# A state-space stage on one core: side work a unit ahead, the product with C written in place

## The chip, the cores and the metric

The kernel runs on one core of one Trainium2 chip. The metric is the time of one execution on the device, in microseconds (us). The core has five engines that run side by side, each taking its instructions strictly in order: TensorE (PE, with its weight loads as PEld), VectorE (DVE), ScalarE (ACT), GpSimd (POOL) and SyncE (SP), which here issues nearly all transfers. They wait for one another through semaphores.

## The reference, cut to what matters

The whole model has four layers. The change touches only the first, a two-level selective state-space block (x is 4 images of 96 channels and 64 x 64 pixels, so sequences of L = 4096; DIN = 192, DSTATE = 16, NLAYERS = 2):

```
for i in range(NLAYERS):
    seq = seq + mamba(seq, ...)
# in mamba, with h the normalized input:
xs, z = split(h @ in_w)
xc    = silu(conv4(xs))                      # causal, 4 taps
dt, Bm, Cm = split(xc @ xproj_w)             # 6, 16, 16 columns
delta = softplus(dt @ dt_w + dt_b)
dA    = exp(delta[..., None] * -exp(A_log))  # L x 192 x 16
dBx   = delta[..., None] * Bm[:, :, None, :] * xc[..., None]
h_t   = dA_t * h_(t-1) + dBx_t               # a scan along L
y     = (einsum('blds,bls->bld', h, Cm) + Dp * xc) * silu(z)
return y @ out_w
```

A fusion by matmul, a batch norm and the residual follow, and then the three other layers (`_back`), whose code is not touched.

## The kernel before, in words

`_mamba` cuts the sequences into chunks of TC = 512 positions. A **unit** is (chunk, level, pair of images), 32 in all, in a fixed list in which a level-1 unit comes three places after the level-0 unit that it reads (units 2 and 31 excepted; they are in `late`, because their input is made only one or two units earlier).

The scan of a unit has 24 **steps** (k, r, h): k = 0..2, r = 0..3, h = 0..1, so step = 8k + 2r + h. Each step treats 2 x 128 rows of (channel, state) pairs, 512 positions long. The loop over the steps writes out by hand, for each engine, the order of its instructions (`manual_schedule`); nothing reorders them later. In step s it issues, in this order:

- `product(s+2)` (line 457, on POOL) if step s+2 is **apart**, that is k < 2, h = 0 and r odd: steps 2, 6, 10 and 14 of a unit. There the input term is loaded (`db`) and multiplied by B on POOL. Then `broadcasts(s+2)` (line 447): otherwise PE spreads delta times x over the states into PSUM (`pq`, three buffers of two banks).
- `reduce` (line 488) in odd steps: PE sums h times C over the states of the step pair finished before, into `py`.
- a **slot** of side work (below).
- `decays(s+3)` (line 452): ACT computes dA = exp(delta A) into tile `a` (six buffers); for an apart step, into `pq`.
- `scans(s)` (line 470): two DVE scans of 512, with DVE's `product(s+1)` (line 457, pq times B) between them unless step s+1 is apart; then POOL's product of the states with C (line 476), from tile `hs` (two buffers, one for each pair of steps) into tile `hc` (two buffers).
- `copies(s+5)` (line 434): SP's transfers of delta, broadcast over 16 partitions of states, from DRAM (`ddl`) into `a`.
- `states` (line 480) in even steps: ACT copies the last column of `hs` to a small tile `hst`, the start of the next chunk's scan. `gate` every 8 steps: y (lines 496, DVE, and 497, POOL).

The **side work** is everything that makes the next units ready. It is a set of Python generators in lanes (class `Side`, lanes front, tail, norm, rest); one call of `slot` lets a lane issue work up to its next `yield`. `yield` alone ends the slot and keeps the lane, "free" lets other lanes in, "gap" asks for at least one slot's distance. `tail(n-1)` projects the finished unit (mm_o, line 369 on), `norm(n+2)` normalizes the input (mm_xc, mm_v, 12 tiny POOL instructions for a reciprocal square root at line 227 on, mm_r at line 240, DVE's `hn` at line 249), and `front(n+1)` is the long chain: mm_i (line 264), Silu, mm_dbl (line 287), three ACT copies (dbl, dh, and dh rounded at line 297), `dx` on POOL (line 303), mm_d, Softplus (line 601), `ddl` to DRAM, `du` on POOL (line 339), copies `ux`/`uy` on ACT (line 352), remainders `ul` on POOL (line 355) and their transfers. All side matmuls share one PSUM bank (`mm`), so each group waits until the group before is copied out.

In the kernel before, `front(n+1)` begins at step 0 of unit n and must be finished at its end: `copies` calls slots in a loop until the next unit is ready, and at step 23 `side.drain()` empties all lanes. In an ordinary unit there is one slot in each step; unit 0 and units before a `late` one have two.

Of the kernel before, what the change touches and what calls it, by code (L numbers as in the profile page):

```python
# [9 lines left out]
F32 = mybir.dt.float32  # L10
# [13 lines left out]
NL = 2  # L24
DS = 16
# [23 lines left out]
def _mamba(ctx, tc, io, w, fd, fstats, xsums):  # L49
# [25 lines left out]

    A, HS, HC = ("a", 0, 2, 6), ("hs", 0, 4, 2), ("hc", 0, 4, 2)

# [10 lines left out]
    fus_w = _load(nc, wp, io["fus_wT"][0:C, :], [C, C], "fus_w")  # L88
    out_wT = staged(io["out_wT"], "out_wT", [C, 2, 128], *HC)
    selF = staged(io["k_sel"].rearrange("c (j m) -> c j m", j=4), "selF", [128, 4, 128], *A)  # L90
# [10 lines left out]

    dtH = stage("dtH", [128, NL, 256], *HC)
    nc.vector.tensor_copy(dtH.bitcast(F32R), dtF)
# [64 lines left out]

    seq, made, ys = {}, {}, {}
    pqs, das, dbs, hss, hcs, pys = {}, {}, {}, {}, {}, {}  # L170

# [17 lines left out]
    def norm(unit):  # L189
# [47 lines left out]
        for n, b in enumerate(bs):  # L237
            p = mm(f"r{n}", unit, [C, TC])
            for j in range(4):
                nc.tensor.matmul(  # L240
                    p[:, j * 128 : (j + 1) * 128],
                    r[:, n * 4 + j : n * 4 + j + 1].to_broadcast([128, C]),
                    ident,
                    start=True,
                    stop=True,
                )
            yield
            yield
            nc.vector.tensor_tensor(hn_buf[b, l][:C, 3:], p, xc[n], ALU.mult)
            yield "free"  # L250

    def front(unit):

        ch, l, pr = unit
        bs = (2 * pr, 2 * pr + 1)
        for j in range(6):
            k = j % 3
            p = mm(f"i{j}", unit)
            taps = [(wk[l][:, t, :], t) for t in range(4)] if j < 3 else [(wz[l], 3)]
            for t, (wt, off) in enumerate(taps):  # L260
                cols = slice(off, off + TC)
                f = dict(start=t == 0, stop=t + 1 == len(taps))
                if k < 2:
                    nc.tensor.matmul(p, wt[:, 0:128], hn_buf[bs[k], l][:, cols], **f)  # L264
                else:
                    for n in range(2):
                        nc.tensor.matmul(p[64 * n : 64 * n + 64], wt[:, 128:DIN], hn_buf[bs[n], l][:, cols], **f)
                if t != 0 and t != 2 or len(taps) == 1:
                    yield
            if j == 0:  # L270
                xcv = tl("xcv", unit, [128, 3, TC], bufs=2)
            if j == 3:
                zs = tl("zs", unit, [128, 3, TC], bufs=2)
            if j < 3:
                nc.scalar.activation(xcv[:, j, :], p, AF.Identity, bias=col(l, 0, k))  # L275
            else:
                nc.scalar.copy(zs[:, k, :], p)
            yield "free"
# [23 lines left out]
        dx = tl("dx", unit, [128, TC], F32R)  # L302
        nc.gpsimd.tensor_tensor(dx, dbl, lo, ALU.add)  # L303
        yield "gap"
        dl = tl("dl", unit, [128, 3, TC])
        bcs = []
        for k in range(3):
# [7 lines left out]
            nc.scalar.activation(dl[:, k, :], p, AF.Identity, bias=col(l, 1, k))  # L315
            if k == 1:
                for at in range(2):
                    t = tl(f"bc{at}", unit, [128, 2, TC], bufs=2)
                    src = ddb[at].rearrange("s n t -> s (n t)")[:, None].to_broadcast([DS, 8, 2 * TC])
                    nc.sync.dma_start(t.rearrange("p n t -> p (n t)"), src)  # L320
                    bcs.append(t)
        _softplus(nc, work, dl)
# [3 lines left out]
        for q in range(4):  # L326
            nc.sync.dma_start(dd[q % 2, :, :, q // 2, :], dl[32 * q : 32 * q + 32])
        us, parts, dus, cut = [], [], [], []
        made[unit] = [xcv, zs, *bcs, dd, us, parts]
        for at in range(6):  # L330
            if at == 2:
                for k in range(2):
# [3 lines left out]
                    us.append(ddu)  # L336
            for k in ((0, 1), (2,))[at] if at < 2 else ():
                dus.append(tl(f"du{k}", unit, [128, TC], to="du", bufs=3))
                nc.gpsimd.tensor_tensor(dus[k], dl[:, k, :], xcv[:, k, :], ALU.mult)
            if at >= 3:  # L340
# [5 lines left out]
                parts.append(cut[at - 3][0:2])  # L346
            while at == 3 and side.step < NS * units.index(unit) - 3:
                yield "gap"
            if 1 <= at < 4:
                cut.append([tl(f"{x}{at}", unit, [128, TC], F32R, to=x, bufs=3) for x in ("ux", "uy")])  # L350
                for t in cut[-1]:
                    nc.scalar.copy(t, dus[at - 1])
            if 2 <= at < 5:
                t = tl(f"ul{at}", unit, [128, TC], F32R, to="ul", bufs=2)
                nc.gpsimd.tensor_tensor(t, dus[at - 2], cut[at - 2][0].bitcast(F32), ALU.subtract)
                cut[at - 2].append(t)
            yield "gap"

    def tail(unit):
# [4 lines left out]
        for n in range(2):  # L364
# [13 lines left out]
            else:  # L378
                ft = work.tile([C, TC], F32, name=f"ft_{tag(unit)}_{n}", tag="ft", bufs=2)
                nc.scalar.copy(ft, p)  # L380
# [5 lines left out]
    def way_out(unit):  # L386
# [11 lines left out]
        for n in range(2):  # L398
            b = 2 * pr + n
            nc.vector.bn_stats(fstats[:, b, ch, :], po[:C, n, :])  # L400
            ft = work.tile([C, TC], F32, name=f"ft_{tag(unit)}_{n}", tag="ft", bufs=2)
            nc.scalar.copy(ft, po[:C, n, :])
# [56 lines left out]
    def scans(s):  # L459
# [3 lines left out]
        if h == 0:  # L463
            hss[g] = scan.tile([128, 4, TC], F32, name=f"hs_{name(s)}", tag="hs")
            hcs[g] = scan.tile([128, 4, TC], F32, name=f"hc_{name(s)}", tag="hc")
        pq, a = pqs.pop(s), das.pop(s)
        d0, d1 = (pq, dbs.pop(s)) if apart(s) else (a, pq)
        for i in (0, 1):
            at = 2 * h + i
            nc.vector.tensor_tensor_scan(  # L470
                hss[g][:, at, :], d0[:, i, :], d1[:, i, :], hst[pr, l, g % 12][:, at : at + 1], ALU.mult, ALU.add
            )
            if i == 0 and s + 1 < n_steps and not apart(s + 1):
                product(s + 1)
        sl = slice(2 * h, 2 * h + 2)
        (nc.gpsimd if s + 1 < n_steps else nc.vector).tensor_tensor(hcs[g][:, sl, :], hss[g][:, sl, :], bc(unit, 3, k, h), ALU.mult)  # L476

    def states(g):
        ch, l, pr = steps[2 * g][0]
        nc.scalar.copy(hst[pr, l, g % 12], hss[g][:, :, TC - 1])  # L480

    def reduce(g):
        unit, k, r, h = steps[2 * g]
        if r == 0:
            pys[unit, k] = ps_y.tile([128, TC], F32, name=f"py_{name(2 * g)}", tag="py")
        hc = hcs.pop(g)
        for i in range(4):
            nc.tensor.matmul(  # L488
                pys[unit, k][32 * (i // 2 + i % 2 * 2) :][:32], red[:, r, :], hc[:, i, :], start=(r == 0), stop=(r == 3)
            )  # L490
# [9 lines left out]
    class Side:  # L500
# [5 lines left out]
        def __init__(self):  # L506
            self.front, self.tail, self.norm, self.rest, self.held, self.step = [], [], [], [], None, 0

        def slot(self):
            waiting = []  # L510
            while True:
                lane = self.held
                if lane is None:
                    lanes = (self.front, self.tail, [] if self.tail else self.norm, self.rest)
                    lanes = [x for x in lanes if x and not any(x is y for y in waiting)]
# [9 lines left out]
                elif got == "end":  # L525
                    lane.pop(0)

        def drain(self):
            while self.slot():
                pass  # L530

    side = Side()
    n_steps = len(steps)
    with tc.manual_schedule():
        for n in (0, 1):
            load(units[n])
        side.front = [weights(0), norm(units[0]), front(units[0])]
        side.drain()
        for s in range(5):
            copies(s)  # L540
# [6 lines left out]
        for s in range(n_steps + NS):  # L547
# [5 lines left out]
            if at == 0:  # L553
                if n + 1 < len(units) and n + 1 not in late:
                    side.front += ([norm(units[n + 1])] if n == 0 else []) + [front(units[n + 1])]
                    side.norm += [weights(1)] * (n == 0)
            if at == 22 and n + 1 == len(units):
# [6 lines left out]
            if n + 2 < len(units) and n + 2 not in late:  # L564
                if at == 8:
                    load(units[n + 2])
                if at == 10:
                    (side.front if n + 1 in late else side.norm).append(norm(units[n + 2]))
            if s + 2 < n_steps:
                unit, k, r, h = steps[s + 2]  # L570
# [9 lines left out]
            side.slot()  # L580
            if n == 0 or n + 1 in late:
                side.slot()
            if s + 3 < n_steps and not apart(s + 3):
                decays(s + 3)
            if live:
                scans(s)
            if live and s + 5 < n_steps:
                unit, k, r, h = steps[s + 5]
                while unit not in made or apart(s + 5) and len(made[unit][5]) <= k:
                    side.slot()  # L590
                copies(s + 5)
            if s % 2 == 0 and 0 < s <= n_steps:
                states(s // 2 - 1)
            if s % 8 == 2 and 2 < s <= n_steps + 2:
                gate(s // 2 - 2)
            if at == NS - 1 and n + 1 < len(units):
                side.drain()

# [955 lines left out]
```

## Time and profile before

| | us |
|---|---|
| three runs before | 5245.57, 5257.07, 5259.77 (median 5257.07) |
| the profiled execution | 5239.08 |
| its span, first to last instruction | 5237.3 |
| before the first scan / the state-space steps / all that follows | 93 / 2991 / 2153 |
| busy in the state-space steps: DVE, POOL, PE, ACT | 2666.7, 2549.8, 2207.8, 1782.6 |
| mean granted clock of TensorE, whole span | 0.819 of full speed |

A unit is 48 scans. In the profile a row such as "L470 DVE TENSOR_TENSOR_SCAN hs<-a,hst,pq ... x1280 | 1575.0, 1263 | 40.1 <-ACT hst L480 17.3" says: line 470 of the kernel, on VectorE, writes hs from a, hst and pq, 1280 times; 1575.0 us busy, 1263 ns each; VectorE was idle for 40.1 us just before these, and most of that ended when ScalarE's line 480 was done. Rows of a timeline are start, duration, engine, line, operation, tiles, count, and in brackets the idle time before with what ended it. Rows of stretches are the stretch, its length, each engine's busy time (with its number of instructions), TensorE's granted clock, the share of the transfer engines that was busy, and GB/s.

### The profile page before, as it was taken

To read this page: it belongs to the slowest core of one execution; us is meant where nothing else is said; L and a number is where in the kernel's file an instruction comes from. 1 tells how busy PE (TensorE), PEld (TensorE's weight loads), DVE (VectorE), ACT (ScalarE), POOL (GpSimd) and SP (SyncE) were. 2 spreads that over 40 slices of the span, in tenths; PEclk is the share of its full clock that TensorE was granted. 3 is DMA by queue.
4 is the path that set the end of the run, shared out by engine and by line. 5 is a ranking of instruction groups with operands and counts; after the bars stand their busy time and mean duration, and the time that the engine had idled before them with its cause. 6 is when DMAs were issued, how large, how long until landed. Compare 5 with 4: busy or idle time off the path is not lost.

```text
span 5237.3 us, 52687 instructions
## 1 busy us (share of the span) xinstructions
PE 4069.8 (78%) x15440; PEld 1747.5 (33%) x15440; DVE 4322.3 (83%) x5639; ACT 2693.7 (51%) x5149; POOL 2988.1 (57%) x2105
## 2 busy tenths in 40 slices
PE   5677777777777777777777637899898899989776
PEld 2222222222222222222222102345455555545565
DVE  2879899898989989899998887879787978787655
ACT  3565666656566665656656520024453544434566
POOL 2878888888888888888888860002130312212122
PEclk7767877777787777778787658999999999999977
DMA  4768888888887888888788765553325233332110
GB/s 100 179 168 192 197 193 205 195 197 195 197 195 192 209 196 193 195 197 202 186 208 196 175 168 157 165 174 94 95 86 155 85 98 97 100 90 79 53 33 21
DMA packets 314046, 800.19 MB, mean 153 GB/s; under 512 B 52247, under 2 KB 58106, under 8 KB 312702
## 3 DMA queue, kind: packets, MB, share of 16 engines
q1 hardware_dynamic: 310174, 790.53, 59.8%
q10 hardware_dynamic: 3584, 6.29, 0.4%
q8 instruction: 123, 2.02, 0.2%
q14 instruction: 165, 1.35, 0.1%
HBM read 703.83 MB, written 67.63 MB: 147 GB/s over the span
## 4 chain that ended last, share of the span: by engine, by line
PE 26%; DVE 24%; issue 15%; POOL 11%; ACT 9%; DMA 7%; SPq 1%; DVEq 0%; POOLq 0%; ACTq 0%
DVE hs L470 10%; PE py L895 10%; DVE pq L457 6%; DMA a<-ddl 5%; POOL hc L476 4%; PE py L488 2%; DVE z L880 2%; ACT a L452 2%; DVE a L1110 2%; PE px L1177 2%; PE ph L1092 2%; PE pa L1078 2%; PE mm_i L264 2%; POOL t L1248 1%; PE pv L1133 1%
## 5 line engine op out<-in xcount | busy, mean ns | idle before, releaser
L476 POOL TENSOR_TENSOR hc<-hs,bc 128x1024 f32<-128x1024 f32 x767 | 1803.2, 2360 | 318.4 <-DVE hs L470 305.7
L470 DVE TENSOR_TENSOR_SCAN hs<-a,hst,pq 128x512 f32<-128x512 f32 x1280 | 1575.0, 1263 | 40.1 <-ACT hst L480 17.3
L895 PE MATMUL py<-z,wk 128*96 128x512 f32 x2304 | 1113.1, 612 | 25.0 <-issue 14.0
L452 ACT ACTIVATE a<-a,aneg 128x512 f32<-128x512 f32 x1280 | 846.1, 711 | 223.4 <-DMA a<-ddl 216.1
L880 DVE TENSOR_TENSOR z<-cp,cp 128x512 f32<-128x512 f32 x1152 | 794.9, 717 | 183.7 <-PE py L895 169.0
L457 DVE TENSOR_TENSOR pq<-pq,bc 128x1024 f32<-128x1024 f32 x640 | 773.2, 1208 | 111.6 <-PE pq L447 111.5
L488 PE MATMUL py<-hc,red 128*32 128x512 f32 x3072 | 672.3, 840 | 39.4 <-POOL hc L476 39.4
L895 PEld LDWEIGHTS py<-z,wk 128*96 128x96 f32 x2304 | 366.9, 169 | 448.7 <-issue 318.9
L447 PE MATMUL pq<-uy,sel 64*128 64x512 f32 x768 | 262.9, 643 | 281.1 <-DVE hs L470 275.1
L470 DVE TENSOR_TENSOR_SCAN hs<-pq,hst,db 128x512 f32<-128x512 f32 x256 | 325.5, 1271 | 148.1 <-POOL dx L303 95.0
L1145 POOL MEMSET zz<- 96x2 f32 x16 | 1.6, 98 | 738.5 <-ACT zz L1154 738.5
L264 PE MATMUL mm_i<-hn,wk 97*128 97x512 f32 x512 | 297.7, 710 | 118.3 <-ACT xcv L275 93.2
L1246 POOL TENSOR_TENSOR o<-o,fb 128x384 f16<-128x384 f16 x64 | 67.0, 1047 | 547.1 <-ACT o L1251 544.1
L452 ACT ACTIVATE pq<-a,aneg 128x512 f32<-128x512 f32 x256 | 177.0, 692 | 343.5 <-DMA a<-ddl 249.3
L457 POOL TENSOR_TENSOR db<-db,bc 128x1024 f32<-128x1024 f32 x128 | 302.0, 2360 | 23.8 <-DMA db<-ddu 23.8
L447 PEld LDWEIGHTS pq<-uy,sel 64*128 64x128 f32 x768 | 97.9, 234 | 568.4 <-DVE hs L470 431.7
L447 PE MATMUL pq<-ux,sel 64*128 64x512 f32 x512 | 181.5, 635 | 96.4 <-DVE hs L470 76.6
L275 ACT ACTIVATE xcv<-mm_i,pvec 128x512 f32<-128x512 f32 x96 | 66.0, 687 | 313.1 <-PE mm_i L264 147.8
L1177 PE MATMUL px<-bd,a 128*96 128x128 f32 x1024 | 148.2, 293 | 67.1 <-DVE a L1110 56.2
L1146 POOL TENSOR_TENSOR zz<-zz 96x256 f32<-96x256 f32 x128 | 122.8, 959 | 133.4 <-ACT zz L1153 81.3
L264 PEld LDWEIGHTS mm_i<-hn,wk 97*128 97x128 f32 x512 | 98.7, 214 | 291.1 <-issue 165.5
L447 PEld LDWEIGHTS pq<-ux,sel 64*128 64x128 f32 x512 | 66.9, 231 | 305.3 <-DVE hs L470 212.0
(286 smaller groups left out, 6534.3 us busy)
## 6 DMA issues: line engine op xcount, KB each, us to landing
a<-ddl SPq DMA_DIRECT2D x768, 512.0 KB, 6.8
cp<-p SPq DMA_DIRECT2D x480, 192.0 KB, 2.7
db<-ddu SPq DMA_DIRECT2D x128, 512.0 KB, 9.0
bc<-ddb SPq DMA_DIRECT2D x64, 512.0 KB, 7.8
cp<-p SPq DMA_DIRECT2D x480, 64.0 KB, 2.7
ddl<-dl SPq DMA_DIRECT2D x128, 192.0 KB, 3.9
tw_k_fwd<-in_k_fwd SPq DMA_DIRECT2D x64, 256.0 KB, 3.4
tw_k_inv<-in_k_inv SPq DMA_DIRECT2D x64, 256.0 KB, 3.1
```

The source lines that it names most:

```text
L264: nc.tensor.matmul(p, wt[:, 0:128], hn_buf[bs[k], l][:, cols], **f)
L447: nc.tensor.matmul(pqs[s][:, i, :], sel[rows, r, :], made[unit][6][k][h][rows], start=True, stop=True)
L452: nc.scalar.activation(to[:, i, :], das[s][:, i, :], AF.Exp, scale=acol(s, i))
L457: engine.tensor_tensor(t, t, bc(unit, 2, k, h), ALU.mult)
L470: nc.vector.tensor_tensor_scan(hss[g][:, at, :], d0[:, i, :], d1[:, i, :], hst[pr, l, g % 12][:, at : at + 1], ALU.mult, ALU.add)
L476: (nc.gpsimd if s + 1 < n_steps else nc.vector).tensor_tensor(hcs[g][:, sl, :], hss[g][:, sl, :], bc(unit, 3, k, h), ALU.mult)
L488: nc.tensor.matmul(pys[unit, k][32 * (i // 2 + i % 2 * 2) :][:32], red[:, r, :], hc[:, i, :], start=(r == 0), stop=(r == 3))
L880: nc.vector.tensor_tensor(zs[n], cps[q, r0], cps[q, r1], ALU.mult)
L895: nc.tensor.matmul(pys[q], wk[k // KG][:, k % KG, :], zs.pop(n), start=(k == 0), stop=(k == NE - 1))
L1078: nc.tensor.matmul(pa[j][:, jj, :], kf[:, 2 * (j % 2) + jj, :], dd[j][:, jj, :], start=True, stop=True)
L1146: nc.gpsimd.tensor_tensor(z0[:, :, 0, :], z0[:, :, 0, :], z1[:, :, 0, :], ALU.add)
L1177: nc.tensor.matmul(p[:, j, :], a2[i % 2][:, kk, :], tabs["bd"][:, int(kk > 0), :], start=True, stop=True)
```

## The change

1. **In place.** `hs` gets 513 columns and three buffers, `hc` is gone. The scans write columns 1 to 512; POOL's product with C reads these and writes columns 0 to 511 of the same tile. The last state stays in column 512 for `states`; `reduce` reads columns 0 to 511.
2. **A unit ahead.** `front(n+2)` is started in unit n, in a new lane `ahead` behind all others, from step 4 on, as soon as both images of `norm(n+2)` are done (`normed`); at the unit's end the lane becomes `front`. Loads and norms start at steps 2 and 4 instead of 8 and 10. `xcv` and `zs` get a third buffer. `side.drain()` at step 23 is gone, and odd steps have two slots.
3. **The chain's last part** (ux, uy, ul, their transfers, bc and ddu) is a generator of its own, `split`, in a lane `low` that goes first, and is spread over the unit before the one that needs it (from its steps 2, 5, 13 and 21).
4. **dx behind the product.** `dx` is not issued at once but put into `side.post` and issued (`flush`) at the next slot or after the step's product with C.
5. `copies` catch up in a loop that remembers how far it came. The tail's ft tiles share sq's buffers.

```diff
+            hss[g] = scan.tile([128, 4, TC + 1], F32, name=f"hs_{name(s)}", tag="hs", bufs=3)
-            hcs[g] = scan.tile([128, 4, TC], F32, name=f"hc_{name(s)}", tag="hc")
...
-                hss[g][:, at, :], d0[:, i, :], d1[:, i, :], hst[pr, l, g % 12][:, at : at + 1], ALU.mult, ALU.add
+                hss[g][:, at, 1:], d0[:, i, :], d1[:, i, :], hst[pr, l, g % 12][:, at : at + 1], ALU.mult, ALU.add
...
-        (nc.gpsimd if s + 1 < n_steps else nc.vector).tensor_tensor(hcs[g][:, sl, :], hss[g][:, sl, :], bc(unit, 3, k, h), ALU.mult)
+        hs = hss[g][:, 2 * h : 2 * h + 2, :]
+        (nc.gpsimd if s + 1 < n_steps else nc.vector).tensor_tensor(hs[:, :, :TC], hs[:, :, 1:], bc(unit, 3, k, h), ALU.mult)
...
     def front(unit):
+        while unit not in normed:
+            yield "gap"
...
-                xcv = tl("xcv", unit, [128, 3, TC], bufs=2)
+                xcv = tl("xcv", unit, [128, 3, TC], bufs=3)
...
-        nc.gpsimd.tensor_tensor(dx, dbl, lo, ALU.add)
+        side.post.append(lambda: nc.gpsimd.tensor_tensor(dx, dbl, lo, ALU.add))
...
+        while side.low:
+            yield "gap"
+        for ks in ((0, 1), (2,)):
+            for k in ks:
+                dus.append(tl(f"du{k}", unit, [128, TC], to="du", bufs=3))
+                nc.gpsimd.tensor_tensor(dus[k], dl[:, k, :], xcv[:, k, :], ALU.mult)
+            if len(ks) == 2:
+                yield "gap"
+        side.low.append(split(unit, ddb, dus, us, parts))
+
+    def split(unit, ddb, dus, us, parts):
+        cut, start = [], NS * units.index(unit) - NS
+        while side.step < start + 2:
+            yield "gap"
...
-            while at == 3 and side.step < NS * units.index(unit) - 3:
+            while at < 4 and side.step < start + 8 * at - 3:
                 yield "gap"
...
-                    lanes = (self.front, self.tail, [] if self.tail else self.norm, self.rest)
+                    lanes = (self.low, self.tail, self.rest, self.front, [] if self.tail else self.norm, self.ahead)
...
+    copied = [5]
...
             if at == 0:
-                if n + 1 < len(units) and n + 1 not in late:
-                    side.front += ([norm(units[n + 1])] if n == 0 else []) + [front(units[n + 1])]
+                side.turn()
...
-                if at == 10:
+                if at == 4:
                     (side.front if n + 1 in late else side.norm).append(norm(units[n + 2]))
+                    side.ahead.append(front(units[n + 2]))
...
-            if n == 0 or n + 1 in late:
+            if n == 0 or n + 1 in late or s % 2 == 1:
                 side.slot()
...
             if live:
                 scans(s)
-            if live and s + 5 < n_steps:
-                unit, k, r, h = steps[s + 5]
-                while unit not in made or apart(s + 5) and len(made[unit][5]) <= k:
+            side.flush()
+            while live and copied[0] < min(s + 6, n_steps):
+                unit, k, r, h = steps[copied[0]]
+                while unit not in made or apart(copied[0]) and len(made[unit][5]) <= k:
+                    if copied[0] > s + 5:
+                        break
                     side.slot()
-                copies(s + 5)
+                else:
+                    copies(copied[0])
+                    copied[0] += 1
+                    continue
+                break
...
-            if at == NS - 1 and n + 1 < len(units):
-                side.drain()
```

The instructions of the two kernels are the same in kind and number on DVE, ACT and POOL; what differs is their order, the tiles and the waits. The steady order of one unit, as it stands on the engines in the changed kernel (steps of unit n; mm_o is of unit n-1; mm_xc to mm_dbl, mm_d, dx, Softplus and du are of unit n+2; ux, uy and ul of unit n+1):

| steps | PE side work | ACT side work | POOL side work |
|---|---|---|---|
| 3, 4 | mm_o, mm_o, mm_xc | copies of both mm_o | y at step 2 |
| 5 to 8 | mm_xc, mm_v | xc, sq, ux, uy, ve, vh, r | Newton (12 small) after step 6's product |
| 9, 10 | mm_r, mm_r | | y (hn on DVE at the end of steps 9 and 10) |
| 11 to 18 | mm_i | xcv, ux, uy, zs, both Silu | ul after step 12's product, y |
| 19 to 21 | mm_dbl, mm_d, mm_d | dbl, dh, dh, ux, uy, dl | dx, ul after step 20's product |
| 22 to 24 | mm_d | dl, dl, Softplus | ul, du, du after step 22's, du before step 24's |

In the kernel before, mm_r stood at steps 21 and 23, mm_i at 0 to 8, mm_o at 9 and 10, both Silu and their table loads between these, mm_dbl at 11 and 12, mm_d at 14 to 16, Softplus at 17, du at 17 and 18, the Newton steps after step 18's product, and ul after the products of steps 19, 20 and 22.

## The prediction

> **What bounds the kernel now.** I read the stretches first. The stretch 400 to 2800 holds the steady units. The columns are its length, the busy time of PE, PEld, DVE, ACT and POOL with instruction counts, TensorE's granted clock, the transfer engines' share and GB/s; the second row counts the scans (line 470) alone, the third those of the start.
>
> ```profile
> 400.00:2800.00 2400.00, 1809.03 (x6116) 564.68 (x6114) 2168.12 (x1927) 1468.77 (x2552) 2086.53 (x1303) 0.76 0.83 197
> ...
> 400.00:2800.00 2400.00, 1537.74 (x1250) 0.76 0.83 197
> ...
> 93.00:400.00 307.00, 171.30 (x139) 0.67 0.73 174
> ```
>
> 1250 scans at 48 to a unit are 26.04 units, so a unit takes 92.2 us; DVE is busy 83.3 of them and POOL 80.1. DVE sets the pace, its 8.9 idle us per unit are all there is to win, and POOL is only 3 us behind it. The waits of DVE in this stretch say who ends these idle times (us in total, times, longest):
>
> ```profile
> DVE hs L470 <- POOL dx L303: 88.8, 26, 4.0
> DVE pq L457 <- PE pq L447: 56.0, 36, 3.2
> DVE hn L249 <- PE mm_r L240: 51.9, 29, 3.7
> DVE hs L470 <- POOL hc L476: 23.1, 24, 1.4
> DVE hs L470 <- issue: 9.2, 16, 1.1
> ```
>
> Over 26 units that is 3.4, 2.15, 2.0, 0.9 and 0.35 us per unit.
>
> The first label misleads. That scan (step 14, apart) doesn't read dx. It writes the `hs` buffer of two step pairs before, which ACT's state copy (line 480) must have read. The timeline of one such place, ACT first, then DVE:
>
> ```profile
> 1659.99 0.58 ACT L293 COPY dbl<-mm_dbl 128x512 f32<-128x512 f32 x1 [3.38 <-PE mm_dbl L290]
> 1660.61 0.62 ACT L295 CAST dh<-dbl 128x512 fp32r<-128x512 f32 x1
> 1661.26 0.72 ACT L297 ACTIVATE dh<-dh,low 128x512 f32<-128x512 f32 x1
> 1661.89 1.32 ACT L452 ACTIVATE a<-a,aneg 128x512 f32<-128x512 f32 x2
> 1663.11 0.18 ACT L480 COPY hst<-hs 128x4 f32<-128x4 f32 x1
> ...
> 1663.38 1.28 DVE L470 TENSOR_TENSOR_SCAN hs<-pq,hst,db 128x512 f32<-128x512 f32 x1 [3.18 <-POOL dx L303]
> ```
>
> ACT stood 3.38 us for mm_dbl, with the state copy queued behind three copies and a decay; the scan starts 0.09 after the copy's end, and dx merely ends at the same moment.
>
> The third label hides the side chain's lateness. PE, in the timeline just before such an `hn`, stands for transfers that the next unit's chain made late, and mm_r is behind it:
>
> ```profile
> 1697.32 0.49 PE L447 MATMUL pq<-ux,sel 64*128 64x512 f32 x1 [0.42 <-DMA ux<-ul]
> ...
> 1699.78 0.79 PE L447 MATMUL pq<-uy,sel 64*128 64x512 f32 x1 [1.89 <-DMA uy<-ul]
> ...
> 1702.36 2.02 PE L240 MATMUL mm_r<-ident,r 128*96 128x128 f32 x8
> ```
>
> The second (pq) is PE's second mm_o, which waits 2.56 for ACT's copy of the first, ACT being behind a Silu and its 1.28 table load.
>
> **The change part by part**, in us per steady unit. Starts of consecutive instructions in the timeline are 1.18 apart for a scan, 1.11 for DVE's product, 0.64 for y or hn, 2.33 for a POOL product of 1024 (rows: 2360 ns), 1.23 for a POOL operation of 512, 3.36 for the twelve Newton ones.
>
> *Work.* Nothing is added or removed in kind. DVE keeps 48 x 1.18 + 20 x 1.11 + 5 x 0.64 = 82.0, with 0.3 of statistics 82.3. POOL keeps 28 x 2.33 + 10 x 1.23 + 3.36 = 80.9.
>
> *In place, 513 columns, three buffers.* The state copy no longer stands between a scan and its buffer, as it has three pairs' time (some 20) instead of two; the hc wait goes too: 3.4 + 0.9 off. The last wait is now db, the decays or pq. DVE's scans take a few more semaphores; the scans behind apart steps have as many today at 1.18, so nothing. Unknown is POOL's product with output one column beside its input. From below: the db product (line 457) is in place already and takes 2360, as the product into hc does, so 0; nothing suggests a gain, as the same elements move. From above: POOL's line 751, two inputs from one tile, takes 1654 against 1191, +39%. The db row is nearest (same size, engine and type); I take 0. At +39% POOL would need 103 and the kernel some 350 slower (10.8 x 32); +9% eats the whole gain below.
>
> [...]
>
> *A unit ahead, split.* mm_dbl moves to step 19, where the sums give 8.4 of work for ACT and PE against 10.5 of DVE time: no stall there. ux, uy and ul are issued 8 steps or more before use, so PE's waits of 0.42 and 1.89 go. Third buffers of xcv and zs cost no time. On SP, the transfers of ux2, ux3 and ddl now stand ahead of `copies` of step 28 and wait for ul and Softplus; the six `a` tiles leave 2 to 3 us of margin, so nothing, but that is thin cover.
>
> *POOL's new order* is what costs. Its instructions from step 22 on are: product 22, ul, du, du, product 23, db(26), du, products 24 to 26, y, product 27, db(30), products 28 to 30, Newton, product 31. That is 12 x 2.33 + 5 x 1.23 + 3.36 = 37.5. PE's reduction of step 31 (1.5) and mm_r (1.6) follow in PE's order before DVE's hn at the end of step 9 (33): 40.6. DVE, from the end of scans 22 to that hn, has eight steps of 2 x 1.18 + 1.11, three of 2.36 (before apart steps) and one y: 35.6. The difference, 5.0, falls on DVE at db(26) (about 1.6), db(30) (0.6) and hn or db(34) (the rest). In the kernel before du, Newton and ul stood at steps 17 to 22, where no db is due, and DVE waited for POOL only 0.9. du also waits for Softplus, behind mm_d, decays and a table load: 0 to 1.5 more; I take 0.2, as du is issued two steps behind it. dx behind the product takes 1.23 out of one step and puts it into the next: 0.
>
> *PE and ACT at steps 3 to 5.* mm_o, its copy, again both, and mm_xc stand between pq and py: 0.8 + 1.0 + 3.08 + 0.9 + 3.08 + 0.9 + 0.7 = 10.5 at full clock, against 11.2 to 11.7 that DVE needs; hidden, by a hair. The pq wait of today (2.15) falls to about 0.8, the part that I give to half clock.
>
> *Sum.* Before 8.8 named: 3.4 + 2.15 + 2.0 + 0.9 + 0.35. After: 5.2 + 0.8 + 0.35 = 6.35. Saved 2.5, so a unit takes 89.7. 27 units (2 to 28) give 68. In the start, 139 scans take 40 us more than at the steady 1.92 a scan, from the same waits in bursts; I give 12. The last three units give 7. The profiled execution, 5239.1 (span 5237.3), would be 5152. The median of the runs is 18 above it, so I forecast **5170**. The 2153 us behind the state-space steps don't change.
>
> **The rivals.**
> *B, more is gained.* The du wait nothing, and DVE's lateness from other waits is the same time in which POOL catches up, so stalls overlap: 3.5 instead of 5.2 in POOL's stretch, a unit of 88.0. For it: POOL idles 12 us a unit today. 4.2 x 27 + 15 + 12 = 140: 5117.
>
> *C, slower: the matmul clump of steps 3 to 5 at half clock.* The trace has both prices: a pq pair takes 0.49 or 0.79, mm_o 3.08 or 4.43, and the stretches around show it:
>
> ```profile
> 1612.00:1652.00 40.00, 29.86 (x106) 8.10 (x106) 39.46 (x36) 24.15 (x39) 36.94 (x17) 0.95 0.98 228
> 1672.00:1692.00 20.00, 13.02 (x47) 5.52 (x46) 19.96 (x18) 16.11 (x29) 16.87 (x21) 0.50 0.75 205
> ```
>
> With 0.50 granted, pq to mm_xc take 15.2, and decays(8) on ACT, queued behind xc, sq and ux, come after 21.5 where DVE needs them at 16.3: 5.2 late, and Newton behind mm_v another 0.5. 2.2 of this overlaps POOL's waits at db(26) and db(30); 89.7 + 3.5 = 93.2, 32 x 1.0 over today: 5289. It decides from 4.7 late per unit. Against it: PE is as busy as before, and the wait for DMA that idled it is gone. A dearer in-place product (above +9%) ends on this side too; I count it here.
>
> [...]
>
> *D, nothing is gained:* the stalls only change name, POOL's stretch taking 7.7 instead of 5.2 (its whole 1.5 for Softplus, and SP's margin used up once). 5257, within 5241 to 5273.
>
> **How the numbers follow.** Forecast 0.47, B 0.25, C 0.15, D 0.13. 0.3% (16 us) is about what a measurement of this kernel can tell from no change. Faster 0.72 (forecast and B), same 0.13 (D), slower 0.15 (C). The range goes down past B for a start that gains more, to 5095, and up to just short of C's centre, 5285; half of C, with the dear product, and B's low end are left out.
>
> **What would show it.** In the changed profile: units 89.7 apart, DVE's busy share in the steady stretch 0.92 to 0.93; no scan that starts right after a state copy; no PE wait for ux or uy transfers; DVE waits for POOL's db at steps 2 and 6 and for mm_r or db at 9 and 10, together about 5 a unit; the in-place product at 2360. Wrong would be: a product above 2450; pq or decay waits above 3 a unit (C); POOL waits below 3.5 (B) or above 7 (D).

## The result, and the profile after

The changed kernel is slower: 5386.23 us (median of 4 runs, 5371.68 to 5396.15) against 5251.32 before, a ratio of 1.0257 (95% interval 1.0223 to 1.029). The forecast was 5170. The profiled execution spans 5369.9 against 5237.3.

The same stretch as in the prediction, 400 to 2800, first all engines (PE, PEld, DVE, ACT, POOL, TensorE's clock, share of the transfer engines, GB/s), then the scans alone, now line 485:

```profile
400.00:2800.00 2400.00, 1763.30 (x5856) 531.21 (x5849) 2071.07 (x1840) 1406.88 (x2440) 1884.45 (x1246) 0.76 0.79 189
...
400.00:2800.00 2400.00, 1461.68 (x1192) 0.76 0.79 189
```

1192 scans instead of 1250 are 24.8 units, 96.6 us each. DVE's share fell from 0.90 to 0.86, where 0.92 to 0.93 was forecast; POOL's from 0.87 to 0.79. The granted clock is 0.76 in both. With the units cut at every 48th scan of the trace:

| us | before | after |
|---|---|---|
| units 0 to 5, together | 597.6 | 638.9 |
| units 6 to 28, mean of one | 92.1 (odd 93.5, even 90.8) | 95.5 (odd 99.2, even 92.2) |
| units 29 to 31, together | 274.5 | 277.1 |

So the 133 us are 41 in the first six units, 79 in the steady ones (23 x 3.4), 3 in the last ones, and 10 around the steps. The waits of DVE in the stretch (us in total, times, longest):

```profile
DVE hn L249 <- PE mm_r L240: 103.7, 25, 5.2
DVE pq L473 <- PE pq L463: 85.7, 55, 6.7
DVE hs L485 <- POOL db L473: 59.9, 25, 3.0
DVE fstats L424 <- ACT ft L396: 43.7, 24, 3.1
DVE hs L485 <- ACT a L468: 23.0, 24, 2.0
```

The two waits that part 1 was to remove are gone: no scan starts behind a state copy, and the wait for POOL's product shows only 0.9 us in all. The new ones are larger: hn 4.2 per unit, pq 3.5, db 2.4, bn_stats (fstats) 3.6 in each odd unit, the decays 0.9. With two small ones they are the 13.2 us that DVE idles per unit (2400 - 2071.07, over 24.8 units).

One odd unit's steps 3 to 9, by the timelines of ACT, PE, POOL and DVE (start, duration, engine, line; in brackets the idle time before and its releaser):

```profile
1419.19 0.31 ACTq L397 DMA_DIRECT2D fd<-ft  x1
...
1427.58 0.63 ACT L205 ACTIVATE xs<-x 96x512 f32<-96x512 f32 x1 [4.60 <-DMA fd<-ft]
...
1429.52 0.57 ACT L197 COPY xc<-mm_xc 96x512 f32<-96x512 f32 x1
...
1436.95 0.28 ACT L225 ACTIVATE r<-ve,magic 128x8 int32<-128x8 int32 x1
...
1420.24 1.09 PE L386 MATMUL mm_o<-y,of_w 64*96 64x512 f32 x2
1421.27 1.10 PE L387 MATMUL mm_o<-s,fus_w 96*96 96x512 f32 x2
...
1430.15 2.02 PE L203 MATMUL mm_xc<-x,ctr 96*96 96x512 f32 x2 [4.59 <-ACT xc L197]
...
1432.93 3.58 PE L214 MATMUL mm_v<-mean,sq 96*128 96x1 f32 x16
...
1442.91 1.92 PE L504 MATMUL py<-hs,red 128*32 128x512 f32 x4 [0.50 <-POOL hs L491]
1444.76 1.66 PE L240 MATMUL mm_r<-ident,r 128*96 128x128 f32 x8
...
1437.32 0.20 POOL L227 TENSOR_TENSOR ra<-r 128x8 f32<-128x8 f32 x1 [5.43 <-ACT hn L234]
...
1440.68 2.17 POOL L491 TENSOR_TENSOR hs<-hs,bc 128x1024 f32<-128x1024 f32 x1
...
1423.02 0.69 DVE L424 BATCH_NORM_STATS2 fstats<-ft 96x6 f32<-96x512 f32 x1 [3.13 <-ACT ft L396]
...
1434.08 2.44 DVE L485 TENSOR_TENSOR_SCAN hs<-a,hst,pq 128x512 f32<-128x512 f32 x2
...
1446.53 0.69 DVE L249 TENSOR_TENSOR hn<-mm_r,xc 96x512 f32<-96x512 f32 x1 [4.48 <-PE mm_r L240]
```

Read it as one chain. ft is written by ACT and sent out at 1419.19. ACT's first pass over x writes its unused output `xs` to the same buffer (sq's, shared since the change) and waits for the end of that transfer, until 1427.58. The copy of mm_xc stands behind it, so PE's second mm_xc is 4.59 late, and mm_v behind that. POOL meanwhile has come to the Newton instructions and stands 5.43 for `r` (the label names hn; Newton reads r, which ended at 1437.23, 0.09 earlier). The states' product of step 7 is queued behind Newton and starts only at 1440.68, though its second scan, the first of the two at 1434.08, ends at about 1435.3; PE's py waits for it, mm_r for py, and DVE for mm_r. Four engines stand in turn, each on an instruction that can't start yet, with other work queued behind it. On POOL some 2.0 of the 5.43, and the 3.36 of Newton itself, held a ready product back; for the rest of the 5.43 that product was not ready either, as its scans had waited for pq.

### The profile page after: what moved, and what is told of

Read it like the earlier page. It is cut to its first block, busy times and chain, and to the rows that moved or that the text cites. A ratio compares the mean times of both kernels' runs of the same rounds, so it can differ in the third digit from the quotient of the medians.

```text
span 5369.9 us, 52754 instructions
## 1 busy us (share of the span) xinstructions
PE 4096.9 (76%) x15440; PEld 1734.8 (32%) x15440; DVE 4322.3 (80%) x5639; ACT 2696.6 (50%) x5149; POOL 2848.8 (53%) x2105
## 3 DMA queue, kind: packets, MB, share of 16 engines
q8 instruction: 123, 2.02, 0.2%
## 5 line engine op out<-in xcount | busy, mean ns | idle before, releaser
L491 POOL TENSOR_TENSOR hs<-hs,bc 128x1024 f32<-128x1024 f32 x767 | 1666.5, 2182 | 454.4 <-DVE hs L485 425.7
L504 PE MATMUL py<-hs,red 128*32 128x512 f32 x3072 | 738.4, 871 | 40.3 <-POOL hs L491 29.3
L463 PE MATMUL pq<-uy,sel 64*128 64x512 f32 x768 | 249.3, 644 | 509.1 <-DVE hs L485 508.9
L463 PE MATMUL pq<-ux,sel 64*128 64x512 f32 x512 | 157.5, 608 | 37.5 <-DMA ux<-ul 21.8
L504 PEld LDWEIGHTS py<-hs,red 128*32 128x32 f32 x3072 | 86.5, 125 | 297.8 <-POOL hs L491 157.2
L268 PEld LDWEIGHTS mm_i<-hn,wk 97*128 97x128 f32 x512 | 114.3, 237 | 202.2 <-issue 158.6
```

What stands on the lines that cost most here:

```text
L463: nc.tensor.matmul(pqs[s][:, i, :], sel[rows, r, :], made[unit][6][k][h][rows], start=True, stop=True)
L504: nc.tensor.matmul(pys[unit, k][32 * (i // 2 + i % 2 * 2) :][:32], red[:, r, :], hc[:, i, :TC], start=(r == 0), stop=(r == 3))
```

## The experiments

Theory P: part 1 is a gain, and the loss comes from the order of the side work, which the doubled slots of the odd steps bunch at steps 3 to 9. Rivals: part 1 costs; the end of the unit (du, ul, Softplus against db) costs; running a unit ahead itself costs. All ratios are to runs of the kernel before on the same chip.

| run | us | ratio, 95% interval |
|---|---|---|
| e1, part 1 alone | 5181.65 | 0.9878 (0.9865 to 0.9892) |
| changed kernel | 5386.23 | 1.0257 (1.0223 to 1.029) |
| e2, ft in s's buffers | 5340.56 | 1.0173 (1.0154 to 1.0191) |
| g1, e2 + Newton three gaps later | 5551.33 | 1.0592 (1.0567 to 1.0617) |
| g2, e2 + bn_stats later | 5331.33 | 1.0163 (1.0131 to 1.0195) |
| g4, e2 + both, and du later | 5400.67 | 1.0299 (1.028 to 1.0319) |
| i1, e2 + Newton behind its step's product | 5301.39 | 1.0106 (1.0072 to 1.014) |
| i2, i1 + bn_stats later | 5281.20 | 1.0066 (1.0044 to 1.0088) |
| h3, e2, doubled up to step 9 only | 5258.57 | 1.0035 (1.0021 to 1.005) |
| h2, e2, doubled from step 10 on only | 5165.82 | 0.9856 (0.984 to 0.9873) |
| g3, e2, one slot | 5153.92 | 0.9819 (0.9802 to 0.9837) |
| h4, g3 + gap in the tail | 5157.74 | 0.984 (0.9825 to 0.9855) |
| h1, changed kernel, one slot | 5148.01 | 0.9822 (0.9799 to 0.9845) |

**Part 1 alone.**

```diff
 (before.py)
-  hss[g] = scan.tile([128, 4, TC], F32, name=f"hs_{name(s)}", tag="hs")
-  hcs[g] = scan.tile([128, 4, TC], F32, name=f"hc_{name(s)}", tag="hc")
+  hss[g] = scan.tile([128, 4, TC + 1], F32, name=f"hs_{name(s)}", tag="hs", bufs=3)
...
-  ...tensor_tensor(hcs[g][:, sl, :], hss[g][:, sl, :], bc(unit, 3, k, h), ALU.mult)
+  ...tensor_tensor(hs[:, :, :TC], hs[:, :, 1:], bc(unit, 3, k, h), ALU.mult)
```

> The kernel before with part 1 alone (513 columns, three state buffers, product in place), order of all instructions as before. Theory P (the loss of the whole change comes from the new order of the side work, part 1 by itself is a gain): the waits of DVE behind the state copy (3.4 us per unit) and behind POOL's product (0.9) go, POOL's product takes about 2180 ns instead of 2360; the side chain's waits (pq 2.15, hn 2.0) stay. Unit about 88.5 to 89.5, time 5130 to 5190. Rival Q (what hides behind the state copy is equally late, so that the wait is only renamed): unit 91.5 or more, 5230 to 5260. Rival R (part 1 is itself the loss): above 5300.

5181.65: a gain of 1.2%, inside P's range for the time; a unit takes 90.2 (2400 / 26.6), a little more than P said. Rival R falls, and Q as it was stated; but part of what Q named, a wait that only changes its name, is there. The waits of DVE in its stretch 400 to 2800:

```profile
DVE pq L457 <- PE pq L447: 130.0, 106, 3.2
DVE hn L249 <- PE mm_r L240: 57.7, 39, 2.2
```

The waits behind the state copy and POOL's product are gone. pq now takes 4.9 per unit (130.0 over 1277 / 48 = 26.6 units) where it took 2.15; hn stays at 2. So of the 4.65 that part 1 frees (3.4, 0.9 and 0.35), 2.75 are taken by the next wait, that for PE's pq behind its side groups, and 2.0 are left.

**The price of POOL's product.** The rows of the page show 2360 ns before (line 476) and 2182 after (line 491). Two kernels take the part of it asunder: states in columns 1 to 512 of a 513 column tile, with the product still going to hc; and in place, unshifted, 512 columns.

> The kernel before, with states in columns 1 to 512 of a 513 column tile, but the product still goes to hc: source shifted, not in place. For the price of POOL's product: 2360 before, 2182 in the changed kernel. If the shift or the odd pitch brings it: about 2180 to 2260. If writing in place brings it: 2360. [...] Time within 1% of the kernel before.

> The kernel before with the product in place and unshifted in a 512 column tile with three buffers (the state handed to the next chunk is then the product, not the state, so the output is not the reference's). For the price of POOL's product: if writing in place brings the 2182, about 2180; if the shift or the pitch brings it, 2360, as the in place row of db has. The time is no matter here, as the state copy now waits for POOL.

The rows of the changed kernel, of e3 and of e4, in this order:

```profile
L491 POOL TENSOR_TENSOR hs<-hs,bc 128x1024 f32<-128x1024 f32 x767 | 1666.5, 2182 | 454.4 <-DVE hs L485 425.7
```

```profile
L476 POOL TENSOR_TENSOR hc<-hs,bc 128x1024 f32<-128x1024 f32 x767 | 1666.2, 2179 | 442.5 <-DVE hs L470 426.4
```

```profile
L475 POOL TENSOR_TENSOR hs<-hs,bc 128x1024 f32<-128x1024 f32 x767 | 1801.6, 2359 | 266.9 <-DVE hs L469 244.5
```

In place costs nothing (2359). What makes the product 8% shorter is the source that starts at column 1 of a 513 column tile, in place or not. Whether the shift against bc or the odd pitch does it was not tried. In e3, time hardly moves (5235.58, one run, before 5245.19): POOL is not the bound there. e4, also one run, takes 5200.70.

**The shared buffer.**

```diff
-  ft = work.tile([C, TC], F32, ..., tag=f"sq{n}", bufs=1)
+  ft = work.tile([C, TC], F32, ..., tag=f"s{b}", bufs=1)   # s is dead once mm_o has read it
```

> The changed kernel, but the tail's ft tiles take the dead buffers of s instead of those of sq; every engine's order is the same. Theory P1 (in the units whose tail is of level 1, ACT's first pass over x writes sq and so waits for the transfer of ft to DRAM; mm_xc, mm_v, Newton and hn are late behind it): the odd units fall from 99.5 to 92 to 93, even ones stay at 91.6, time 5386 - 14 x 7 = about 5290 (5270 to 5320). Rival P2 (the clump of matmuls and the doubled slots set the lateness, the transfer only fills a time that PE needs anyway): less than 2 us per odd unit, 5360 or more.

Between P1 and P2: 46 us less. The odd units fall from 99.2 to 95.7, about half of what P1 expected, and the even ones rise from 92.2 to 92.9; bn_stats and hn still wait in the odd ones. With ACT's wait for the transfer goes the half clock of mm_xc: of the 44 matmuls of mm_xc in the odd units 7 to 27, 21 took more than 0.9 us in the changed kernel (0.59 is the shortest), and 1 in e2.

**Newton and bn_stats.** These were to remove two single waits by three more gaps each; in g4 both, with three more gaps ahead of du.

```diff
   nc.scalar.activation(r.bitcast(I32), ...)
+  for _ in range(3):
+      yield "gap"
   for _ in range(3):          # Newton
```

```diff
 def rest(ch, fts):
+    for _ in range(3):
+        yield "gap"
     for b, ft in fts:
```

> e2, with three more gaps ahead of the twelve Newton instructions, which so stand behind step 8's product on POOL instead of step 6's (the side chain behind them two steps later too). Theory N (Newton is issued on POOL before mm_v and ACT's r can be there, POOL stands 3.8 us per unit with product 27 behind it, and so py, mm_r and hn are late): POOL's wait at ra falls below 0.5 and DVE's hn wait from 4.2 to below 2, time 5340 - 27 x 2.2 = about 5280 (5250 to 5300). Rival M (mm_r is late by what stands ahead of it on PE in any order): hn wait above 3, time 5320 or more.

> e2, with three more gaps ahead of bn_stats of the tail's ft tiles, nothing else moved. Theory S (DVE stands 3.6 us in each odd unit for bn_stats, as the lane rest now goes ahead of front and bn_stats is issued in the step in which mm_o is copied): the wait for ft goes, and 2 to 3.6 of it are gained, 5340 - 15 x 3 = about 5295 (5285 to 5315). Rival T (the 3.6 only stand in for POOL's lateness, and hn or pq wait longer instead): above 5325.

> e2 with Newton (as in g1) and bn_stats (as in g2) later, and three more gaps ahead of du, which so stands behind step 4's product of the next unit instead of 22's. If the three waits add up as theories N and S say, and the db wait of step 2 (2.4) goes with du: 5340 - 60 - 45 - 50 = about 5190 to 5230. If they stand in for one another: 5270 or more.

All three are misses. g2 gains 9 us, inside its noise, and its steady units take what they take in e2 (94.3 against 94.2, units 6 to 28): the fstats wait is gone and the pq wait of the odd units takes its place (rival T). g1 loses 211 us. POOL no longer waits at Newton, but the gaps shift the whole chain behind it into another place: mm_d, Softplus and du fall into steps 0 and 1 of the next unit, and most of mm_o runs at half clock (233 of its 276 matmuls in units 6 to 28 take more than 0.9 us, 4 in the changed kernel). The stretch 400 to 2800 of g1 (granted clock 0.69), and one mm_o there, 2.02 a pair where the changed kernel has 1.10:

```profile
400.00:2800.00 2400.00, 1821.70 (x5550) 527.04 (x5549) 1963.87 (x1742) 1342.59 (x2319) 1782.27 (x1183) 0.69 0.74 178
```

```profile
1476.28 2.02 PE L388 MATMUL mm_o<-y,of_w 64*96 64x512 f32 x2 [0.71 <-POOL y L515]
1478.22 2.02 PE L389 MATMUL mm_o<-s,fus_w 96*96 96x512 f32 x2
```

So g1 and g4 tell nothing on Newton's place. A gap in a generator moves everything behind it.

**One slot in odd steps.**

```diff
-  if n == 0 or n + 1 in late or s % 2 == 1:
+  if n == 0 or n + 1 in late:
       side.slot()
```

> e2, with one slot of side work in odd steps too, as in the kernel before: mm_o, mm_xc, mm_v, mm_r stand one to a step, Newton behind step 12's product, du behind 14's, and the chain of unit n+2 runs on into unit n+1 (mm_i to du there). Theory K (the bunching of the side work by doubled slots at steps 3 to 9 and 19 to 24 makes the waits, the run ahead does not): all of db, hn, fstats and pq together fall from 10 to about 5, as in e1 (7.4 idle): 5180 to 5240. Rival L (the work ahead itself, with its place in the first units, costs): 5290 or more.

> The changed kernel with one line undone: one slot in odd steps (ft still in the buffers of sq). Theory K (the doubled slots make the loss, the shared buffer costs only where the tail and the next norm stand close together): mm_o now stands in step 5 and x's first pass in step 6 or later, so the transfer of ft has some 4 to 8 us; time 5154 to 5190 (e2 with one slot took 5154). Rival (the shared buffer costs its 4 us per odd unit in any order): 5154 + 14 x 3.3 = 5200.

g3 went below what K expected: 187 us less than e2. h1 undoes only this line of the change and takes 5148.01, 238 us less than the changed kernel; with and without the shared buffer the time is the same, so the transfer of ft costs only where x's first pass comes right behind it. h1's scans and DVE's waits in 400 to 2800:

```profile
400.00:2800.00 2400.00, 1595.96 (x1305) 0.76 0.86 206
```

```profile
DVE pq L473 <- PE pq L463: 140.7, 84, 9.1
DVE hn L249 <- PE mm_r L240: 4.1, 2, 2.4
```

1305 scans are 27.2 units of 88.3. No wait for db, bn_stats or the decays is left, and of hn 4.1 us in all; pq takes 5.2 per unit, at the same clock of 0.76. Most of the gain over the kernel before is that of part 1, which by itself has a ratio of 0.9878 (e1); the rest of the change at one slot, the run ahead with it, adds 0.6% (0.9822). Units 0 to 5 take 594.5, so the 41 us of the start are gone as well. One slot also moves each group to another step: mm_r stands where DVE is at steps 9 and 10 in e2, and at 16 to 19 in g3. How much is the bunching, and how much the place, these two runs don't tell.

**Which clump.**

```diff
-  if n == 0 or n + 1 in late or s % 2 == 1:
+  if n == 0 or n + 1 in late or s % 2 == 1 and at >= 10:     (h2)
+  if n == 0 or n + 1 in late or s % 2 == 1 and at < 10:      (h3)
```

> e2 with the second slot in odd steps only from step 10 on: mm_o, mm_xc, mm_v and mm_r stand one to a step and Newton behind step 8's product, while mm_i to mm_d stay as dense as in the changed kernel. Theory K1 (the clump of tail and norm at steps 3 to 9 is what costs): 5170 to 5220. Rival K2 (the clump at the unit's end, Softplus, du and ul against db of steps 26 and 30, costs): 5280 or more.

> e2 with the second slot in odd steps only up to step 9: tail and norm as dense as in the changed kernel, the long chain one to a step (so it runs over into steps 0 to 8 of the next unit, and du falls beside db(30)). K1: 5300 or more. K2: 5170 to 5220.

h2 is just under K1's range (5165.82), h3 between K1 and K2 (5258.57). The waits of DVE of h2, then of h3:

```profile
DVE pq L473 <- PE pq L463: 61.6, 24, 4.2
DVE hn L249 <- PE mm_r L240: 57.4, 27, 5.6
DVE hs L485 <- POOL db L473: 44.7, 34, 2.7
```

```profile
DVE hs L485 <- POOL db L473: 121.5, 51, 4.8
DVE pq L473 <- PE pq L463: 65.8, 36, 7.3
DVE hn L249 <- PE mm_r L240: 43.2, 26, 3.4
```

Of the 187 us between e2 and g3, the density at steps 3 to 9 takes 175 if it is removed alone (h2), that at the unit's end 82 (h3). The two are not additive, and in h3 du has moved ahead of the db of step 10, and the db wait is 4.7 per unit. The tail and norm clump is the larger one.

**Newton's place alone.** What carries the lateness in the clump? Here the order of PE, ACT and DVE stays as in e2; the twelve instructions go behind the product of their step.

```diff
+  def newton():
       for _ in range(3):
           nc.gpsimd.tensor_tensor(a, r, r, ALU.mult)
           ...
+  side.post.append(newton)
```

> e2 with one thing moved: the twelve Newton instructions go behind the product of their step on POOL instead of ahead of it (through the list that dx uses); the orders of PE, DVE and ACT are the same. In the changed kernel POOL stood at Newton until about 1437.3 and the product behind it began at 1440.7, so PE's py of that pair and mm_r behind it began at 1444.8. Theory N (this place is what makes hn late): the product runs while ACT makes r, Newton ends at the same time, POOL's wait at ra falls from 3.8 to some 1.5 and DVE's hn wait from 4.2 to 1.5; time 5340 - 27 x 2.7 = 5267 (5250 to 5295). Rival N2 (mm_r would come as late behind mm_v and Newton alone): hn wait above 3, 5320 or more.

> i1 with bn_stats three gaps later as well. If N holds and the pq wait that g2 showed in the place of the fstats wait stays: within 15 of i1. If the 3.6 of bn_stats only stood before the hn wait: 5215 to 5250.

i1 takes 5301.39, 39 us less than e2, a little past N's range. POOL's wait at Newton in the stretch, in the changed kernel, in e2 and in i1:

```profile
POOL ra L227 <- ACT hn L234: 93.9, 25, 5.5
```

```profile
POOL ra L227 <- ACT hn L234: 62.7, 25, 4.5
```

```profile
POOL ra L228 <- ACT r L225: 1.8, 1, 1.8
```

DVE's wait at hn, in e2 and in i1:

```profile
DVE hn L249 <- PE mm_r L240: 109.3, 25, 8.7
```

```profile
DVE hn L252 <- PE mm_r L243: 50.9, 22, 3.4
DVE hn L252 <- ACT a L471: 9.7, 4, 2.4
```

The shared buffer made a part of POOL's wait, which is 3.8 a unit in the changed kernel and 2.5 in e2; in i1 it is gone, and hn's wait falls from 4.3 to 2.3. So theory N holds for about half of hn. Moving bn_stats as well (i2) is 20 us less in the median, more than the 15 that were expected if pq takes over; but the steady units take the same in both (92.5, units 6 to 28), with the pq wait up from 57.3 to 100.6 in the stretch, and the difference lies in the units before and behind them and in what follows. The 127 us that are left between i2 and g3 go with the doubled slots and the places that come of them. Candidates are mm_o, mm_o and mm_xc in one step ahead of pq, two mm_r close together, and du ahead of db; they weren't taken apart, so this part is not explained.

**A version better than both.** The rest in g3 is pq, 5 us per unit.

```diff
-  yield "free"                      # between the two mm_o of a tail
+  yield "gap" if n == 0 and ... else "free"
```

> For a version better than both: e2 with one slot (5154), and a gap between the two mm_o of a tail, which stand in one step together there. What is left in the run with one slot are pq waits of 4 to 6 us per unit, 0.2 to 3.7 each. If the two mm_o in one step make them: some 1 to 2 us per unit less, 5090 to 5130; if mm_xc and mm_dbl behind ACT's Silu make them: 5145 to 5165.

5157.74: nothing gained, so not the two mm_o. In h1's trace PE stands 131.1 us in the stretch for ACT's xc ahead of mm_xc, with mm_dbl behind it, and 44.4 for transfers of ux; which of them makes pq late was not tried. The fastest are h1 and g3, which their intervals don't tell apart; h1 is 1.8% faster than before and 4.4% than the changed kernel.

## Why the prediction was wrong

**Right.** The wait labelled dx was the state copy, and part 1 removes it and the product's wait: e1 shows it, and no such wait stands in the profile after. The in-place product costs nothing (2359 in e4, 2360 before). db waits at step 2, as forecast, with 2.4 instead of 1.6: the forecast took 0.2 for Softplus ahead of du, and POOL idles 1.2 for it in each steady unit.

**Wrong, the step that failed:** "mm_o, its copy, again both, and mm_xc stand between pq and py: ... = 10.5 at full clock, against 11.2 to 11.7 that DVE needs; hidden, by a hair", and with it Newton as 3.36 of POOL work that is ready when POOL gets there. The sum took each engine's clump by itself. The clump is a chain through four in-order queues: PE's mm_xc waits for ACT's copy, ACT's pass for a transfer, POOL's Newton for ACT's r, PE's py for the product behind Newton. POOL stood 3.8 per unit at Newton, where the sum had 0 (2.5 without the shared buffer, in e2); from there i1 gives 39 us back by moving those twelve instructions by one product. hn's 4.2 per unit is thus not POOL being full: POOL's busy share fell. In the terms of the sum, 6.35 of waits were forecast and 13.2 measured: pq 3.5 for 0.8, POOL's db and hn together 6.6 for 5.2, bn_stats 1.8 for nothing, the decays 0.9 for nothing. Which queue makes the larger part of this late stays open, as said above; that the second slot of the odd steps makes it is shown (h1).

**A label misread.** hn's wait before, 2.0 per unit, was put down to PE's waits for transfers of ux and uy, which the change was to remove. PE's waits for them in the same stretch of the kernel before:

```profile
PE pq L447 <- DMA ux<-ul: 5.0, 11, 1.0
PE pq L447 <- DMA uy<-ul: 1.9, 1, 1.9
```

That is 6.9 us in 26 units, and the 1.89 of the place that the prediction shows came once. It can't make 2.0 in each unit; what did was not looked for. (By its own terms the 35.6 of DVE in POOL's stretch is 35.5, which changes nothing.)

**Not priced at all:** ft in sq's buffers, named in the description of the change but counted as nothing. This transfer out held its buffer for 8.4 us (1419.19 to 1427.58), and ACT's next writer of the buffer stood in front of all its other work: 46 us (e2). bn_stats was costed as 0.3 of work, with no question of when ft is ready; lane `rest` had moved ahead of front, and DVE waited 3.6 in each odd unit. Removing that wait alone gains nothing clear of noise (g2), as pq is late next.

**The start:** 12 us were to be gained, 41 were lost; with one slot units 0 to 5 take 594.5, 3 less than before.

**Rival C** had the place (steps 3 to 5), and gave 5289 for it. Its price was the matmuls' half clock. The clock after is 0.76, as before, and the mm_o of the odd unit shown stand at 1.10 a pair, full clock; in units 6 to 28, 4 of the 276 matmuls of mm_o took more than 0.9 us, and 66 in the kernel before. mm_xc and mm_v are at half clock (2.02 and 3.58, granted clock 0.50 from 1430 to 1440 and 1.00 from 1420 to 1425) behind PE's 4.59 idle, and mm_xc returns to full clock when ACT's wait for the transfer is taken away (in e2, 1 of the 44 in the odd units takes more than 0.9 us, against 21). So for mm_xc the clock followed the wait and did not make it; mm_v in the odd units stays at 0.35 us each in e2, as it is in units 6 to 28 of the kernel before. At the place shown, the first mm_xc, at 1423.04, took 1.10, and the second, behind the 4.59 of idle, 2.02.

**Unforeseen on the other side:** POOL's product became 0.18 shorter, 4.3 per unit. The ten products in POOL's stretch of 37.5 are thus 1.8 shorter than I summed: the forecast's 5.0 stood on a row that the change itself altered.

The forecast of 89.7 per unit was near to the kernel without the doubled slots: h1 takes 88.3. That is in part luck, since h1's waits are not those of the sum: db and hn are gone, and pq takes 5.2 where 0.8 was forecast. One line of the change, which I read as "two slots in odd steps" and gave no cost, made the whole difference of sign.

## What to carry to other kernels

When side work is moved in a hand-written order, price the chain through the queues: for each moved instruction ask whether its input is ready when its engine reaches it, and what ready work stands behind it; sums of work per engine hide this. In this kernel running ahead paid only with the issue rate left as low as the deadline allowed: the same change with one slot a step was 1.8% faster than before (1.2% of it from part 1 alone), and with two in the odd steps 2.6% slower. Ask of a buffer that a transfer reads when its next writer comes: here the writer was held until 8.4 us after the transfer's issue (1419.19 to 1427.58), and ft in other buffers took 46 us less (e2).

## What the runs showed of the hardware that was not expected

- POOL's product of 128 x 1024 f32 takes 2.36 us from a 512 column tile and 2.18 from columns 1 to 512 of a 513 column tile (e3, e4), in place or not. The shifted product is 8% shorter, where the prediction took no change. DVE's scans that write the shifted columns take 1.26 as before.
- A transfer of 192 KB to DRAM, issued by ACT at 1419.19 in the changed kernel, released its source only by 1427.58.
- Three gaps in one generator (g1) brought the mean granted clock of the stretch from 0.76 in e2 to 0.69, and the kernel took 4% longer than e2.
